# A graph network of two layers on one core: stores of the heads stage on another queue, later constants, ordered loads, and one empty step

## The chip, the cores and the metric

The kernel runs on one NeuronCore of a Trainium2 chip. All times are device microseconds (us) of one execution; the time of a kernel is the median of its runs. The engines are TensorE (PE in the profile, with its weight loads as PEld), VectorE (DVE), ScalarE (ACT), GpSimd (POOL) and SyncE (SP), which issues transfers between the main memory and the on-chip memory. ScalarE can issue transfers too; its transfers stand in a queue of its own.

## What is computed

The input is x, 128 graphs of 128 nodes with 256 channels, and an adjacency matrix for each graph. Layer 0 normalizes x, applies a convolution of width 1 and one of width 17 along the nodes, a message step over soft edges, and a gated update; layer 1 applies five small graph convolutions to groups of the first 25 nodes. Cut to what matters:

```python
h = relu(layernorm(x))
# layer 0
c = relu(bn1(conv1(h)))                  # width 1
c = bn2(conv2(c))                        # width 17, pad 8
x_conv = relu(c + h)
s = h @ w_se.T + b_se
A = exp(-dist(s, s)) * adj
x_nmp = A @ relu(h @ w_msg.T + b_msg)
r, z, n = gates(concat(x_conv, x_nmp), h)  # as in a GRU cell
x = x + (1 - z) * n + z * h
# layer 1: for five groups of nodes, two graph convolutions each
x = x + fused(relu(layernorm(x)), adj)
```

## The kernel before

The 128 graphs are taken in 32 blocks of four (BB = 4, NBLK = 32). The work has three stages.

**Heads** (about 0 to 277 us). The convolution of width 17 is done by a transform along the nodes. Here the weights' spectra are computed (`weight_spectra`, matmuls in line 172), 16 of them, each of four steps, and each written to the tensor `vd` in main memory (line 182, 2176 KB). Beside them run the 32 blocks: load x into a buffer `ln` (line 189, four buffers), statistics (`head_stats`, lines 199 to 205, with a power on GpSimd), normalization (`head_norm`, line 211), transposes and relu (`head_turn`, lines 221 and 222, then a store of the result `ht` to `htd[i]`, line 223), the first convolution (`head_conv1`, matmuls in line 235, bias in line 238), and the spectra of the block (`head_spectra`, line 251, copied to `X`, lines 259 and 261). In this stage the order of every engine is the order of the text (`manual_schedule`). The function `heads` writes this order out; `between()` in it is one step of the weights' spectra. PSUM has eight banks, which this stage takes in rotation: a matmul group can start when the reader of the group eight places before it is done. Constants come from the generator `constants()`: its first part scales the first batch normalization, its second folds it into the weights, its third (`scales(1, ...)`, lines 127 to 132, and line 145) scales the second one. The third part is asked for ahead of `heads`, as are the normalization of block 1 and the statistics of block 2.

**Spectral product** (277 to 457 us). For 68 frequencies p, `spectral` multiplies X by the spectra (lines 321 and 326), after a sum on GpSimd (line 318). The spectra come back from `vd` for four frequencies at a time, in two tiles `v` (line 300, 1024 KB each, five buffers). Results are stored by ScalarE to `yd` and `yrd`. From p = 20 on, every fourth p also calls `gate_steps`, which takes one step of `gate_loads` (the loads of the weights `wms`, `idm`, `bms`, `whh` and `wih` for the next stage, lines 436 to 443) and, at some p, one step of the sums that GpSimd does on these weights. The engines other than GpSimd are ordered by a scheduler here, which may place a load earlier than its text stands.

**Gates** (457 to 1891 us). For each block, `gates` does 28 gate products (line 652; each is two passes per matmul in the profile), with a call of `step()` after each. Steps alternate between the generator `beside_gates(i + 1)`, which prepares the next block, and the second layer's generators. `beside_gates` runs, one piece for each step: the messages (line 538, two pieces), the inverse transform (`conv_out`, two pieces: four matmuls on 16 rows each in line 513 and products in line 517, added to `xc` by VectorE in line 520), the edges' terms, the edges (line 588), the messages' sum (`x_nmp`, line 603), and beside these the pieces of `back(i - 2)` (the end of an earlier block: lines 793 to 834). What is left of it is done in a hook near the end of the gate products. Each product takes one of the eight PSUM banks. VectorE's readers of the products are lines 657 to 673, those of the messages lines 548 to 557.

Of the kernel before, what the change touches and what calls it, by code (L numbers as in the profile page):

```python
# [13 lines left out]
P = 128  # L14
# [12 lines left out]
MW = 130  # L27
# [47 lines left out]
def gnn_kernel(ctx: ExitStack, tc: tile.TileContext, io, out0: bass.AP, out1: bass.AP):  # L75
# [21 lines left out]
    def row(name, n):  # L97

        return bass.AP(tensor=io[name].tensor, offset=io[name].offset, ap=[[0, P], [1, n]])
# [65 lines left out]
    def weight_spectra(pool, c, q, w2):  # L165

        sp = pool.tile([P, LW, WCH], F32, tag="sp", name="sp", bufs=2)
        for t in range(WCH // 8):
            ps = [bank() for _ in range(4)]
            for j in range(2):  # L170
                for r in range(4):
                    nc.tensor.matmul(ps[r][:, j * LW:(j + 1) * LW], w2[32 * r:32 * r + KW, 2 * t + j, :],  # L172
                                     gt[32 * r:32 * r + KW, :], start=True, stop=True)
            for r in range(4):
                o0 = t * 8 + 2 * r
                dst, s = sp[:, :, o0:o0 + 2], ps[r][:, :2 * LW].rearrange("p (j d) -> p d j", j=2)
                if r == 3 and t < WCH // 8 - 1:
                    nc.vector.tensor_copy(dst, s)
                else:
                    nc.scalar.copy(dst, s)  # L180
            yield
        nc.scalar.dma_start(vd[c, q], sp)


    xs, stats, hcs, h1s = {}, {}, {}, {}
# [28 lines left out]
    def head_turn(wk, i):  # L214

        ln = xs.pop(i)
        ht = wk.tile([P, C, T], F32, tag="ht", name="ht", bufs=2)
        for c in range(C):
            ps = bank()
            for b in range(BB):  # L220
                nc.tensor.transpose(ps[:, b * N:(b + 1) * N], ln[:, b, c * P:(c + 1) * P], ident)  # L221
            nc.scalar.activation(ht[:, c, :], ps, AF.Relu)
        nc.scalar.dma_start(htd[i], ht)
        hcs[i] = ht

    def head_conv1(wk, i, h):
# [13 lines left out]
    def head_relu(i, h):  # L240
        hv = h1s[i][:, 2 * h:2 * h + 2, :]
        nc.scalar.activation(hv, hv, AF.Relu)
# [18 lines left out]
                        nc.scalar.copy(dst, s[:, d0:d1])  # L261
                    d0 = d1

    def heads(wk, xk, ahead, X, between):

        for i in range(NBLK + 1):
            if i + ahead < NBLK:
                head_load(xk, ahead, i + ahead, nc.sync)
            if i < NBLK:
                head_conv1(wk, i, 0)  # L270
            between()
            if i < NBLK:
                head_relu(i, 0)
            if i + 3 < NBLK:
                head_stats(wk, i + 3, (0,))
            if i < NBLK:
                head_conv1(wk, i, 1)
            if i + 1 < NBLK:
                head_turn(wk, i + 1)
            if i < NBLK:  # L280
                head_relu(i, 1)
            if i + 2 < NBLK:
                head_norm(i + 2)
            between()
            if i > 0:
                head_spectra(X, i - 1)
            if i % 8 == 7:
                between()
            if i + 3 < NBLK:
                head_stats(wk, i + 3, (1,))  # L290

    def spectral(bp, X, p_from, p_to, amid):

# [68 lines left out]
    with front as es:  # L362
        hk = es.enter_context(tc.tile_pool(name="hk", bufs=1))
        xp = es.enter_context(tc.tile_pool(name="xp", bufs=1))
        X1 = xp.tile([P, C, NP_ - NB, 2, P], F32)
        order = es.enter_context(ExitStack())
        order.enter_context(tc.manual_schedule(engines={nc.gpsimd.engine}))
        early = es.enter_context(ExitStack())
        xe = early.enter_context(tc.tile_pool(name="xe", bufs=1, side="right"))
        X0 = xe.tile([P, C, NB, 2, P], F32)  # L370
        X = X0, X1
        with ExitStack() as ws:

            ws.enter_context(tc.manual_schedule())

            xk = ws.enter_context(tc.tile_pool(name="xk", bufs=1, side="right"))
            wp = ws.enter_context(tc.tile_pool(name="wp", bufs=1))
            ahead = 4
            todo = [(c, q) for c in range(C) for q in range(D // WCH)]
            nc.scalar.dma_start(gt, io["gt"])  # L380
            nc.scalar.dma_start(vec, io["vec"])

            taps = [taps_load(wp, *todo[0], nc.sync, split=4, amid=[lambda: head_load(xk, ahead, 0, nc.sync)])]
            spectra = []

            def some_spectra(k=1):
                for _ in range(k):
                    if not spectra and todo:
                        spectra.append(weight_spectra(wp, *todo.pop(0), taps.pop(0)))
                    if spectra and next(spectra[0], STOP) is STOP:  # L390
                        spectra.pop(0)
                        if len(todo) > 2:
                            taps.append(taps_load(wp, *todo[2], nc.sync))
                        some_spectra()

            constant_loads()
            head_load(xk, ahead, 1, nc.sync)
            taps.append(taps_load(wp, *todo[1], nc.sync))
            for k in range(2, ahead):
                head_load(xk, ahead, k, nc.sync)  # L400
            nc.sync.dma_start(fw, row("fw", 5))
            taps.append(taps_load(wp, *todo[2], nc.sync))
            consts = constants()
            next(consts)
            head_stats(hk, 0)
            some_spectra()
            next(consts)
            head_norm(0)
            some_spectra()
            some_spectra()  # L410
            head_turn(hk, 0)
            head_stats(hk, 1)
            some_spectra()
            head_norm(1)
            head_stats(hk, 2)
            next(consts)
            heads(hk, xk, ahead, X, some_spectra)
            while spectra or todo:
                some_spectra()
        turns.close()  # L420
        banks[:] = [ctx.enter_context(tc.tile_pool(name="psum", bufs=8, space=bass.MemoryType.PSUM, reuse_waits="tile")), None]

        bp = es.enter_context(tc.tile_pool(name="bp", bufs=1, reuse_waits="tile"))
        spectral(bp, (X0, 0), 0, NB, {})
        early.close()
        gw = ctx.enter_context(tc.tile_pool(name="gw", bufs=1, side="right", reuse_waits="tile"))
        idm = gw.tile([P, N], F32)
        wms = gw.tile([P, C, 2, MW], F32)
        bms = gw.tile([P, 2, MW], F32)
        swm = gw.tile([P, 3, MW], F32)  # L430
        wih = gw.tile([P, 2 * C, 3 * D], F32)
        whh = gw.tile([P, C, 3 * D], F32)
        sw = [gw.tile([P, 3, 3, P], F32, name=f"sw{k}") for k in range(3)]

        def gate_loads():
            nc.sync.dma_start(wms, io["wms"].rearrange("(c p) (q o) -> p c q o", p=P, q=2))
            yield
            nc.sync.dma_start(idm, io["idm"])
            nc.sync.dma_start(bms.rearrange("p q o -> p (q o)"), row("bms", 2 * MW))
            for name, w in (("whh", whh), ("wih", wih)):  # L440
                for c in range(w.shape[1]):
                    yield
                    nc.sync.dma_start(w[:, c], io[name][c * P:(c + 1) * P])

        loads, sums = gate_loads(), gate_weights()

        def gate_steps(p):
            next(loads, None)
            if p in (36, 40, 44, 52, 56, 60, 64):
                next(sums, None)  # L450

        amid = {p: lambda p=p: gate_steps(p) for p in range(NB, NP_, 4)}
        spectral(bp, (X1, NB), NB, NP_, amid)
        for _ in sums:
            pass
        order.close()
# [540 lines left out]
    def beside_gates(i):  # L997

        ends = back(i - 2, *back_loads(i - 2)) if i > 1 else iter(())
        if i < NBLK:  # L1000
            parts = messages(i)
            next(parts)
            yield
            next(parts)
            next(ends, None)
            yield
            inverse = conv_out(i) if i else iter(())
            next(inverse, None)
            next(ends, None)
            yield  # L1010
            edge_terms(i)
            next(ends, None)
            yield
            for _ in inverse:
                yield
            edges(i)
            yield
            next(ends, None)
            yield
            yield  # L1020
            yield from x_nmp(i)
        for _ in ends:
            yield
            if i == NBLK:
                yield
# [210 lines left out]
```

## Time and profile before

| | |
|---|---|
| median of 3 runs | 1885.14 us (1882.31 to 1886.73) |
| the profiled execution | 1892.84 us, its span 1891.0 us |
| TensorE busy | 1863.2 us (99%) |
| VectorE, ScalarE, GpSimd busy | 1359.9, 745.7, 666.6 us |
| moved by transfers | 267.98 MB, mean 142 GB/s |
| in the heads stage (100 to 200 us) | 312 GB/s, DMA share 0.86 |
| in the spectral stage (380 to 390 us) | 305 GB/s, DMA share 0.90 |
| a gates block without layer 1 | 37.1 us |

"Busy" counts a matmul from its start to its end, so TensorE can be busy and yet wait inside a row of matmuls. The profile names, for an idle stretch, the instruction whose end came last before it (the releaser). The chain of waits follows the last instruction back to what released it. The granted clock is a share of TensorE's full clock.

### The profile page before, as it was taken

Reading aid. Unit: us, or ns where it says so; the run is one execution under the profiler, and the core shown is the slowest. Engines: PE = TensorE matmul, PEld = TensorE weight load, DVE = VectorE, ACT = ScalarE, POOL = GpSimd, SP = SyncE. Lnnn points to the kernel's source line nnn. Section 1 sums busy time; section 2 is a strip of 40 time slices with the busy share of each in tenths; the row PEclk is TensorE's granted clock in tenths of the full one; section 3 lists DMA queues with packets and bytes.
Section 4 is the critical chain, followed back from the end, with each engine's and each line's share of the span. In section 5 each row is a group of like instructions: output and inputs, shape, how many; then the busy total and the mean of one; then the engine's idle time right before and its main releaser. Section 6 shows DMA issues by size and latency. Waiting matters only on the chain.

```text
span 1891.0 us, 31451 instructions
## 1 busy us (share of the span) xinstructions
PE 1863.2 (99%) x10982; PEld 1601.9 (85%) x10982; DVE 1359.9 (72%) x3312; ACT 745.7 (39%) x1667; POOL 666.6 (35%) x803
## 2 busy tenths in 40 slices
PE   7999999999999999999999999999999999999998
PEld 6888888888888888888788888888788888888787
DVE  6878865455978888888656778887666778888643
ACT  4666651111443334333444433433343343334334
POOL 1111125575344544354312345444312244544200
PEclk8999999999999999999999999999999999999999
DMA  7888778996533233324234432334233333232125
GB/s 264 303 314 318 295 280 281 333 312 236 177 91 76 72 82 90 76 74 111 72 101 113 121 76 71 84 83 111 63 102 97 120 90 84 72 71 69 39 88 155
DMA packets 219421, 267.98 MB, mean 142 GB/s; under 512 B 106211, under 2 KB 182968, under 8 KB 217216
## 3 DMA queue, kind: packets, MB, share of 16 engines
q1 hardware_dynamic: 207167, 195.61, 37.3%
q10 hardware_dynamic: 12096, 70.36, 9.0%
q8 instruction: 88, 1.44, 0.3%
q14 instruction: 70, 0.57, 0.1%
HBM read 169.24 MB, written 96.67 MB: 141 GB/s over the span
## 4 chain that ended last, share of the span: by engine, by line
PE 92%; DMA 3%; DVE 2%; POOL 1%; issue 0%; ACT 0%; SPq 0%; ACTq 0%; DVEq 0%; POOLq 0%
PE bank L652 45%; PE bank L235 6%; PE bank L326 5%; PE bank L980 5%; PE bank L920 5%; PE bank L538 5%; PE bank L517 3%; PE bank L251 3%; PE bank L603 3%; PE bank L321 3%; PE bank L172 2%; PE bank L513 2%; PE bank L221 1%; PE bank L899 1%; PE bank L829 1%; DMA v<-vd 1%
## 5 line engine op out<-in xcount | busy, mean ns | idle before, releaser
L652 PE MATMUL bank<-t,sw 128*128 128x256 f32 x1152 | 291.1, 380 | 0.0
L665 POOL TENSOR_TENSOR u<-u,m 128x256 f32<-128x256 f32 x128 | 94.1, 735 | 499.7 <-ACT m L663 421.4
L652 PEld LDWEIGHTS bank<-t,sw 128*128 128x128 f32 x1152 | 210.6, 190 | 26.7 <-issue 2.3
L652 PE MATMUL bank<-t,wih 128*128 128x256 f32 x768 | 197.2, 379 | 0.0
L652 PEld LDWEIGHTS bank<-t,wih 128*128 128x128 f32 x768 | 143.4, 190 | 19.3 <-DVE u L670 0.5
L235 PE MATMUL bank<-wc,ht 128*128 128x256 f32 x512 | 128.9, 397 | 0.9 <-ACT sp L180 0.9
L318 POOL TENSOR_TENSOR vs<-v 128x256 f32<-128x256 f32 x134 | 98.2, 756 | 76.3 <-PE bank L321 41.3
L561 ACT ACTIVATE msg<-msg 128x512 f32<-128x512 f32 x64 | 37.0, 623 | 207.4 <-DVE msg L557 207.3
L652 PE MATMUL bank<-xc,wih 128*128 128x256 f32 x384 | 117.1, 386 | 0.0
L980 PE MATMUL bank<-w,hh 128*125 128x256 f32 (+9 forms) x480 | 113.8, 380 | 1.9 <-DVE hh L925 1.9
L652 PE MATMUL bank<-t,whh 128*128 128x256 f32 x384 | 114.5, 380 | 0.0
L652 PE MATMUL bank<-xn,wih 128*128 128x256 f32 x384 | 114.2, 379 | 0.0
L235 PEld LDWEIGHTS bank<-wc,ht 128*128 128x128 f32 x512 | 95.6, 196 | 17.1 <-ACT sp L180 1.1
L205 POOL TENSOR_TENSOR rs<-ve,mhalf 128x4 f32<-128x4 f32 x32 | 32.3, 1008 | 220.3 <-DVE ve L203 216.5
L652 PE MATMUL bank<-ht,whh 128*128 128x256 f32 x384 | 109.9, 380 | 0.0
L920 PE MATMUL bank<-ax,w 128*128 128x500 f32 (+8 forms) x416 | 107.0, 396 | 0.1
L980 PEld LDWEIGHTS bank<-w,hh 128*125 128x125 f32 (+9 forms) x480 | 84.3, 178 | 20.4 <-DVE hh L925 2.7
L698 ACT ACTIVATE nn<-nn,vec 128x512 f32<-128x512 f32 x64 | 46.3, 724 | 138.5 <-DVE nn L697 138.5
L315 DVE SCALAR_TENSOR_TENSOR s<-X 128x256 f32<-128x256 f32 x67 | 44.8, 670 | 69.9 <-PE bank L326 69.9
L670 DVE TENSOR_TENSOR u<-bank,u 128x256 f32<-128x256 f32 x128 | 53.5, 418 | 53.9 <-PE bank L652 53.5
L180 ACT COPY sp<-bank 128x272 f32<-128x272 f32 x208 | 66.9, 402 | 55.5 <-PE bank L172 53.9
L920 PEld LDWEIGHTS bank<-ax,w 128*128 128x128 f32 x416 | 69.9, 190 | 19.4 <-issue 12.1
(206 smaller groups left out, 4458.6 us busy)
## 6 DMA issues: line engine op xcount, KB each, us to landing
vd<-sp ACTq DMA_DIRECT2D x16, 2176.0 KB
v<-vd SPq DMA_DIRECT2D x34, 1024.0 KB
w<-in_w_dram SPq DMA_DIRECT2D x40, 512.0 KB
ln<-in_x_dram SPq DMA_DIRECT2D x32, 512.0 KB
htd<-ht ACTq DMA_DIRECT2D x32, 512.0 KB
yd<-ys ACTq DMA_DIRECT2D x32, 512.0 KB
ht<-htd SPq DMA_DIRECT2D x32, 512.0 KB
ym<-yd SPq DMA_DIRECT2D x32, 512.0 KB
```

The costliest lines, as they stand in the source:

```text
L180: nc.scalar.copy(dst, s)
L235: nc.tensor.matmul(pv[:, bb, :], ht[:, c, b * N:(b + 1) * N], wc1[:, c, :], start=c == 0, stop=c == C - 1)
L251: nc.tensor.matmul(ps[:, bb * LW:(bb + 1) * LW], h1[:, 2 * h + bb, c * P:(c + 1) * P], fd, start=True, stop=True)
L318: nc.gpsimd.tensor_tensor(vs[:, c], vr[c], vi[c], op=ALU.add)
L321: nc.tensor.matmul(p1[:, :D], a[:, c], vs[:, c], start=c == 0, stop=c == C - 1)
L326: nc.tensor.matmul(ps[:, k * D:(k + 1) * D], u[:, c], w[c], start=c == 0, stop=c == C - 1)
L517: nc.tensor.matmul(ps[:, b * N:(b + 1) * N], ym[:, 2 * h + b, o * P:(o + 1) * P], idm, start=False, stop=b == 1)
L538: nc.tensor.matmul(ps[:, b, :], d[:, b * N:(b + 1) * N], w, start=True, stop=True)
L652: nc.tensor.matmul(ps, w, d, start=n == 0, stop=n == len(pairs) - 1)
L665: nc.gpsimd.tensor_tensor(got["u4"], got["u2"], got["m5"], op=ALU.add)
L920: nc.tensor.matmul(pv[:, q - q0, :], w1s[k5 + g][:, c, q * P:(q + 1) * P], xv[:, c], start=c == 0, stop=c == C - 1)
L980: nc.tensor.matmul(ps[:n1, :D], hh[:, q, at:at + n1], w2s[k5 + g][:, q, :], start=q == 0, stop=q == HID // P - 1)
```

## The change

Four edits. The stores of the spectra and of `ht` in the heads stage are issued by SyncE in place of ScalarE. The normalization of block 1, the statistics of block 2 and the third part of the constants move from ahead of `heads` into it: into block 0, and (the constants) to the end of block 2; with that, the statistics of block 3 are done in one piece at the end of block 0. The loads of the gate weights are kept in the order of the text among SyncE's instructions. And `beside_gates` has one more step that does nothing, ahead of the first piece of `conv_out`.

```diff
@@ weight_spectra, head_turn @@
-        nc.scalar.dma_start(vd[c, q], sp)
+        nc.sync.dma_start(vd[c, q], sp)
...
-        nc.scalar.dma_start(htd[i], ht)
+        nc.sync.dma_start(htd[i], ht)
@@ heads @@
-    def heads(wk, xk, ahead, X, between):
+    def heads(wk, xk, ahead, X, between, consts):
...
-            if i + 3 < NBLK:
+            if i == 0:
+                head_norm(1)
+            elif i + 3 < NBLK:
                 head_stats(wk, i + 3, (0,))
             if i < NBLK:
                 head_conv1(wk, i, 1)
...
             if i < NBLK:
                 head_relu(i, 1)
+            if i == 0:
+                head_stats(wk, 2)
             if i + 2 < NBLK:
                 head_norm(i + 2)
             between()
...
             if i + 3 < NBLK:
-                head_stats(wk, i + 3, (1,))
+                head_stats(wk, i + 3, (1,) if i else (0, 1))
+            if i == 2:
+                next(consts)
@@ the caller of heads @@
             some_spectra()
-            head_norm(1)
-            head_stats(hk, 2)
-            next(consts)
-            heads(hk, xk, ahead, X, some_spectra)
+            heads(hk, xk, ahead, X, some_spectra, consts)
@@ gate_loads @@
+        def gate_load(to, what):
+            tc.keep_in_program_order(nc.sync.dma_start(to, what))
+
         def gate_loads():
-            nc.sync.dma_start(wms, io["wms"].rearrange("(c p) (q o) -> p c q o", p=P, q=2))
+            gate_load(wms, io["wms"].rearrange("(c p) (q o) -> p c q o", p=P, q=2))
             yield
...
             for name, w in (("whh", whh), ("wih", wih)):
                 for c in range(w.shape[1]):
                     yield
-                    nc.sync.dma_start(w[:, c], io[name][c * P:(c + 1) * P])
+                    gate_load(w[:, c], io[name][c * P:(c + 1) * P])
@@ beside_gates @@
             next(parts)
             next(ends, None)
             yield
+            yield
             inverse = conv_out(i) if i else iter(())
             next(inverse, None)
```

More of the change, by code (lines that the diff above doesn't have):

```diff
@@ L433, in gnn_kernel @@
         sw = [gw.tile([P, 3, 3, P], F32, name=f"sw{k}") for k in range(3)]
+        def gate_load(to, what):
+            tc.keep_in_program_order(nc.sync.dma_start(to, what))
         def gate_loads():
-            nc.sync.dma_start(wms, io["wms"].rearrange("(c p) (q o) -> p c q o", p=P, q=2))
+            gate_load(wms, io["wms"].rearrange("(c p) (q o) -> p c q o", p=P, q=2))
             yield
-            nc.sync.dma_start(idm, io["idm"])
-            nc.sync.dma_start(bms.rearrange("p q o -> p (q o)"), row("bms", 2 * MW))
+            gate_load(idm, io["idm"])
+            gate_load(bms.rearrange("p q o -> p (q o)"), row("bms", 2 * MW))
             for name, w in (("whh", whh), ("wih", wih)):
```

## The prediction

> **What bounds the kernel now.** The page first: its busy table says that TensorE is the bound, with 27.8 us of the span in which it does nothing. So a change can win only in those 27.8 us, or where TensorE is busy but slower than it could be. The waits of TensorE, and of its weight loads, come next.
>
> ```profile
> PE 1863.2 (99%) x10982; PEld 1601.9 (85%) x10982; DVE 1359.9 (72%) x3312; ACT 745.7 (39%) x1667; POOL 666.6 (35%) x803
> ...
> PE bank L321 <- POOL vs L318: 3.3, 1, 3.3
> PE bank L513 <- DMA yr<-yrd: 3.0, 1, 3.0
> PE bank L172 <- DVE h L238: 2.9, 1, 2.9
> ...
> PEld bank L652 <- DVE nh L667: 9.2, 26, 0.4
> PEld bank L513 <- DVE u L660: 7.6, 23, 0.3
> ```
>
> Columns: us in total, times, longest. Three single waits of 3 us stand beside two small ones that come once in nearly every block. The small ones hardly show in TensorE's busy time, because a matmul held up counts as busy. Third, the chain of waits around the single ones (start, us, what), and the table of stretches for the granted clock.
>
> ```profile
> 22.87 1.00 POOL rs L205
> 23.88 0.68 POOL bnrs L129
> ...
> 25.21 0.61 DVE h L238
> ...
> 25.86 1.29 PE bank L172 x16
> 27.15 3.71 PE bank L235 x8
> ...
> 37.44 2.05 PE bank L251 x16
> 39.49 1.73 PE bank L235 x8
> ```
>
> ```profile
> 340.21 11.63 DMA v<-vd
> ...
> 351.91 0.73 POOL vs L318
> ...
> 353.38 3.36 PE bank L326 x8
> ```
>
> After each idle stretch the same work takes twice as long: L235 x8 3.71 us against 1.73 at 39.49, L326 x8 3.36 against 1.73 in the steady chain. The stretches 26 to 37 and 353 to 357 us have a granted clock of 0.55 and 0.57. Fourth, the timeline of TensorE around line 513, in block 1 and in a block of the middle, and the chain after it:
>
> ```profile
> 485.15 0.71 PE L513 MATMUL bank<-idr,yr 16*128 16x256 f32 x8
> ```
>
> ```profile
> 1109.11 1.06 PE L513 MATMUL bank<-idr,yr 16*128 16x256 f32 x8
> ```
>
> ```profile
> 1119.12 3.25 PE bank L652 x14
> ```
>
> The same eight instructions take 0.71 us where their four PSUM banks are free and 1.06 where one waits for VectorE's line 660: 0.35 us lost. L652 x12 is 2.59 us everywhere, so x14 should be 3.02; here it is 3.25, the wait for line 667: 0.23 us.
>
> [...] This run shows 0.33 us of ScalarE for a store, and nothing yet on both kinds in one queue. [...]
>
> **Heads' stores by SyncE.** Removed from ScalarE: 32 + 16 issues of 0.33 us, 16 us. No wait of TensorE for ScalarE in this stage exceeds 1.1 us in all, so this is worth 0. Added on SyncE: the same issues, and two waits. Store htd(i+1) waits for the relu of block i+1 (about 1.1 us after its transposes); behind it is the x load of block i+5, released by those transposes: 1.5 us later. vd was complete one step earlier, so it doesn't block. In the queue, though, the load can stand behind htd 0.52, vd 2.23 and taps 0.52 MB: with its own 0.52, 3.8 MB; at 310 to 430 GB/s (measured in the stage and at 255 to 258 us) 8.8 to 12.2 us, after 1.5 us. VectorE's stats need it 13.7 us after the transposes (93.2 to 106.9 us), and TensorE stands it 1.3 us longer (h of line 238 ends at 101.1, its bank is needed at 102.4). It fits, hardly. At the end, the second v load waits behind htd of block 31: 268.7 instead of 265.5 us, needed at 277. I take 1 us lost; bounds 0 and the slower rival.
>
> **Second constants behind the first blocks.** Up to 21.9 us nothing moves on TensorE. VectorE now runs h(0,0) at 19.4 (conv1 just done) to 20.0, a copy to 20.4, norm(1) (1.38) to 21.8, h(0,1) to 22.5, stats(2) with ve (2.3) to 24.9, POOL's pow to 26.0, norm(2) to 27.4, copy to 27.75, stats(3) to 30.1, h(1,0) to 30.7. TensorE, at full clock: transposes of block 1 to 22.9, L172 to 23.6, L235 to 25.35, L172 to 26.0, L235 to 27.95, L221 to 28.85. The next L172 takes the bank that h(1,0) reads: 1.9 us idle, to 30.7; then 31.4; L251 needs h(1,1), at 32.7 (half a stats and 0.6 us later), and ends at 34.3. Before, it ended at 39.49: 5.2 us gained. What is late next is VectorE, with stats of blocks 2 and 3 in a row. The scales moved to the end of block 2 cost VectorE about 2.4 us there (bnve to brz, 22.70 to 25.12); h(3,0) is then at 46.2, its bank wanted at 47.4: hidden, and up to 1 us if not. Bounds: 7.9 us without the idle 1.9 and 0.8; 0 if 1.9 us idle halves the clock again as long as before (it lost 5 us).
>
> **Gate weights' loads in text order.** In the program as built, the second whh load and the first wih load leave the place ahead of the second v of step 28, and the other three wih loads go one to each group of four steps. That v can't start earlier (its buffer is released by step 23, at 340.2). Two loads of 0.39 MB ahead of it at 400 GB/s are 2.0 us, so 11.63 becomes 9.6; TensorE starts at 350.6 instead of 352.7, idle 1.2 us against 3.3 and with no halved clock. The three wih loads issued at 344.5 to 349.2 also shared these 11.6 us, so it may be all of it. Value of all: 3.3 idle, plus 0.27 (L321 x2 0.70 for 0.43) and 1.63 (L326) and 0.05: 5.3. I take 4.7; bounds 2.1 and 5.3. The spread loads add 1.0 us of DMA to each 10.4 us group, in which a tenth is free (share 0.88 to 0.90 from 370 to 400 us). The sums on GpSimd come at step 40 and later: hidden.
>
> **The empty step.** It puts line 513 behind two more gate products (12 L652, 2.6 us). Its four banks are then those that VectorE lines 660, 555, 556 and 557 read; in the block at 1109 us these end by 1110.3, and line 513 comes at 1111.8: no wait. Gain 0.35 x 23 = 8.0 us. Next the banks of the second half: line 520 for it now comes after n2, the statistics of line 819 and hn, by my sums at 1117.0 to 1117.8; the first matmuls of nn that take its bank come at 1118.4: no wait either, and line 667's bank is no longer taken there. Gain 0.23 x 25 = 5.8. The edges' bank (hn's) is free at 1117.0, wanted at 1117.4. Twelve steps of the generator instead of eleven still fit in the thirteen ahead of the hook. So 13.8; bounds: 16 (the three longer waits at 817, 893 and 1333 us, 0.7 each, also gone), and -5 if a wait of 0.6 comes with each of 30 blocks in place of these.
>
> **Sum.** 5.2 + 4.7 + 13.8 - 1.0 = 22.7 us. Own time of the profiled execution 1892.84 (span 1891.0 and 1.8 around it), so 1870.1; it lay 7.7 us over the median 1885.14, and the same change of the median gives 1862.4.
>
> **Rivals.** (a) The wait at line 513 only moves: the margins of 0.4 to 0.6 us at hn's and line 520's banks are eaten by ScalarE, which must copy n1 and relu xc first. Against: five of six margins are larger. Then 8.9 us are left: 1876. (b) The idle 1.9 us at 29 us halves the clock and the v load stays late: 5.2 and 2.6 us less, 1870. (c) Slower: stores and loads in one queue. From the point where an x load comes 15.0 us or later after its buffer's transposes, each us is TensorE's; at 3 us for 14 of 16 vd stores, 42 us: 1885 + 42 - 23 = 1904. For it: the DMA share is 0.82 to 0.86 in this stage. Against: the sums above. It decides over the rest from 1.6 us for each store. (d) The change does little: the steady waits are filled by others and the single ones return elsewhere: 1885.
>
> **Numbers.** Forecast 0.62, (a) 0.20, (b) 0.08, (c) 0.07, (d) 0.03. 0.2% (3.8 us) is about what a measurement of this kernel can tell from no change. Faster 0.90, same 0.03, slower 0.07. Range 1855 (7.9 + 5.3 + 16 gives 1856) to 1877, which takes in (a) and (b).
>
> **What would show it.** Line 513 x8 at 0.7 us in all blocks and no row of its weight loads for line 660; L652 x14 at 3.02 us; the first L251 ending near 34 us, clock 1.00 from 26 to 37; no PE wait for POOL at line 321. Wrong if PE or VectorE waits for x loads at line 199 before 260 us, or if line 588, 652 or 829 shows a new wait in 20 blocks and more. The wait for yr at 462 us stays.

## The result, and the profile after

The changed kernel takes 1865.39 us (median of 4 runs, 1865.10 to 1866.29) where the kernel before takes 1885.33 in the runs beside it: ratio 0.9897, 95% interval 0.9880 to 0.9914, 19.9 us less. In a second comparison, with other runs of both, the ratio was 0.9901 (0.9886 to 0.9916). The forecast was 1862.4, in a range of 1855 to 1877. The changed kernel's profiled execution spans 1864.5 us and is 0.9 us above its median; the one before spans 1891.0 and lay 7.7 above. The profiled spans therefore differ by 26.5 us, 6.6 more than the medians.

Lines 321, 326, 513, 588, 652, 667 and 829 of before are lines 327, 332, 519, 594, 658, 673 and 835 of after. The busy table of the changed kernel:

```profile
PE 1843.8 (99%) x10982; PEld 1592.3 (85%) x10982; DVE 1361.9 (73%) x3312; ACT 737.0 (40%) x1668; POOL 652.9 (35%) x803
```

TensorE is still the bound and runs the same 10982 instructions, but it is "busy" for 19.4 us less: most of what went was hidden in busy time. Its idle time fell only from 27.8 to 20.7 us. The waits of TensorE in the changed kernel (us in total, times, longest):

```profile
PE bank L519 <- DMA yr<-yrd: 3.2, 1, 3.2
...
PE bank L172 <- DVE h L238: 2.0, 1, 2.0
PE bank L251 <- DVE h L238: 1.0, 2, 0.6
```

No row for POOL at line 327: the stall at step 28 (frequency p = 28 of the spectral product) is gone. The wait for yr stays. The front still waits for h, now in three pieces. The timeline of TensorE in the changed kernel (start, us, and in brackets the idle time before, with what ended it) shows the front and one block of the middle:

```profile
31.50 0.74 PE L172 MATMUL bank<-gt,w 17*128 17x136 f32 x16 [1.96 <-DVE h L238]
...
33.50 3.09 PE L251 MATMUL bank<-fd,h 128*128 128x136 f32 x12 [0.59 <-DVE h L238]
...
42.60 2.12 PE L251 MATMUL bank<-fd,h 128*128 128x136 f32 x16
```

```profile
1131.96 0.71 PE L519 MATMUL bank<-idr,yr 16*128 16x256 f32 x8
```

The reader is to see two things. Line 519 takes 0.71 us also in the middle of the run, where it took 1.06. And twelve L251 take 3.09 us after two short idle times, while sixteen take 2.12 at 42.60: the clock is halved again behind the idle 1.96 and 0.59 us (granted 0.50 from 33.45 to 36.86 us). The chain of waits of the changed kernel (start, us, what) confirms the steady blocks:

```profile
1095.50 0.64 PE bank L519 x8
...
1110.77 10.36 PE bank L658 x48
...
1132.03 0.64 PE bank L519 x8
```

48 products in 10.36 us are 0.216 each, the undisturbed price: the wait of 0.23 us for the bank of line 667 is gone too. From one line 519 to the next are 36.53 us; before it was 37.09. One sign that the prediction named for being wrong is there, on VectorE: the statistics of line 199 wait for x loads, which in the kernel before they never did:

```profile
DVE st L199 <- DMA ln<-in_x_dram: 2.9, 3, 1.2
```

TensorE has no wait between 60 and 270 us, so these waits stay hidden.

### The profile page after: what moved, and what is told of

It is laid out like the page before. It is cut to its first block, busy times and chain, and to the rows that moved or that the text cites. A ratio compares the mean times of both kernels' runs of the same rounds, so it can differ in the third digit from the quotient of the medians.

```text
span 1864.5 us, 31417 instructions
## 1 busy us (share of the span) xinstructions
PE 1843.8 (99%) x10982; PEld 1592.3 (85%) x10982; DVE 1361.9 (73%) x3312; ACT 737.0 (40%) x1668; POOL 652.9 (35%) x803
## 4 chain that ended last, share of the span: by engine, by line
PE 90%; DVE 4%; DMA 2%; POOL 2%; SPq 1%; issue 1%; ACT 1%; ACTq 0%; DVEq 0%; POOLq 0%
PE bank L658 43%; PE bank L332 6%; PE bank L235 6%; PE bank L926 5%; PE bank L986 5%; PE bank L544 4%; PE bank L251 4%; PE bank L523 3%; PE bank L327 3%; PE bank L609 3%; PE bank L172 2%; PE bank L221 1%; PE bank L905 1%; DMA nt<-in_adjN_dram 1%; PE bank L835 1%; PE bank L519 1%
## 5 line engine op out<-in xcount | busy, mean ns | idle before, releaser
L235 PE MATMUL bank<-wc,ht 128*128 128x256 f32 x512 | 126.0, 390 | 0.0
L235 PEld LDWEIGHTS bank<-wc,ht 128*128 128x128 f32 x512 | 93.8, 193 | 15.1 <-issue 0.3
L986 PEld LDWEIGHTS bank<-w,hh 128*125 128x125 f32 (+9 forms) x480 | 84.3, 178 | 18.8 <-DVE hh L931 1.0
L669 ACT COPY m<-bank 128x256 f32<-128x256 f32 x128 | 47.3, 369 | 104.5 <-PE bank L658 104.5
L926 PEld LDWEIGHTS bank<-ax,w 128*128 128x128 f32 x416 | 69.9, 190 | 19.4 <-issue 12.3
```

Of the source, the lines that this page charges most:

```text
L235: nc.tensor.matmul(pv[:, bb, :], ht[:, c, b * N:(b + 1) * N], wc1[:, c, :], start=c == 0, stop=c == C - 1)
L926: nc.tensor.matmul(pv[:, q - q0, :], w1s[k5 + g][:, c, q * P:(q + 1) * P], xv[:, c], start=c == 0, stop=c == C - 1)
L986: nc.tensor.matmul(ps[:n1, :D], hh[:, q, at:at + n1], w2s[k5 + g][:, q, :], start=q == 0, stop=q == HID // P - 1)
```

## The experiments

Twelve runs. First each part alone on the kernel before, then each of three parts taken out of the changed kernel, then second looks and doses. The state of knowledge when each expectation was written is in its text. They were made in three comparisons of four kernels, each with its own runs of the kernel before (medians 1885.14, 1887.40 and 1886.36 us), against which the ratios stand.

### Stores alone

```
-        nc.scalar.dma_start(vd[c, q], sp)
+        nc.sync.dma_start(vd[c, q], sp)
-        nc.scalar.dma_start(htd[i], ht)
+        nc.sync.dma_start(htd[i], ht)
```

> The kernel before with the heads' two kinds of store given to SyncE and nothing else. Theory (the three other parts each remove a wait of their own, and the stores are worth nothing): within 2 us of the kernel before, no wait of line 199 for x loads, the second v load of step 28 as late as before (TensorE idle about 3.3 us at line 321). Rival 1 (the stores carry a part of the gain, because ScalarE is free of 48 issues): 3 us or more faster, with fewer waits of TensorE for ScalarE between 40 and 270 us. Rival 2 (stores and loads in one queue cost something that the other parts hide): 3 us or more slower.

Measured 1885.41 us, ratio 0.9998 (0.9991 to 1.0005). The theory holds on the time. Two of its details fell. VectorE waited for x loads at line 199, 3.4 us in 4 times, though TensorE did not wait between 60 and 270 us. And the second v load wasn't "as late as before": this execution waited only 0.5 and 0.7 us for POOL at line 321, the first sign that this stall isn't the same in each execution.

### Constants alone

The diff's edits in heads and in what calls it, nothing else; its core:

```
-            head_norm(1)
-            head_stats(hk, 2)
-            next(consts)
...
+            if i == 2:
+                next(consts)
```

> The kernel before with the second constants behind the first blocks and nothing else. Theory: the first L251 ends at 36 to 37 us instead of 39.5, TensorE idle 1.9 to 2 us at line 172 and again 0.6 us at line 251, clock down to about 0.8 from 30 to 40 us; 2 to 3.5 us faster. Rival (the place at the front is a gain only because the stores have left ScalarE): the first L251 ends at 38 us or later, less than 1.5 us faster.

Measured 1888.98 us, ratio 1.0016 (1.0006 to 1.0025): slower, which neither theory expected. The timeline of TensorE in this kernel:

```profile
32.83 3.09 PE L251 MATMUL bank<-fd,h 128*128 128x136 f32 x12 [0.59 <-DVE h L238]
...
41.85 1.43 PE L251 MATMUL bank<-fd,h 128*128 128x136 f32 x10
```

```profile
349.83 1.02 PE L327 MATMUL bank<-vs,X 128*128 128x256 f32 x2 [2.63 <-POOL vs L324]
350.64 1.91 PE L332 MATMUL bank<-v,s 128*128 128x256 f32 x4
```

(The view of the second group ends after ten of its sixteen matmuls.) The front does what the theory said: the first L251 ends at 35.9. But the second group of L251 (the 17th, of block 1) starts at 41.85. In the first profile of before it started at 45.30, but in three other executions with the old front and the stores on ScalarE it starts at 41.82, 42.43 and 42.91, and in two with the old front and the stores on SyncE at 40.62 and 40.69. So the new front is earlier only against that first profile. Why this kernel is slower, and not merely the same, isn't shown. At step 28 this execution has a long stall with a halved clock behind it (1.91 us for four L332, 1.03 elsewhere).

### Gate loads alone

The diff's gate_load and its uses, nothing else:

```
+        def gate_load(to, what):
+            tc.keep_in_program_order(nc.sync.dma_start(to, what))
```

> The kernel before with the gate weights' loads in text order and nothing else. Theory: no wait of TensorE for POOL at line 321, TensorE busy throughout from 340 to 360 us at full clock, 4.5 to 6 us faster. Rival (the loads only fit because the stores and the front have moved the time of the spectral steps against the transfers): a wait of 1 us or more stays at line 321 or at line 326, less than 3 us faster.

Measured 1882.38 us, ratio 0.9984 (0.9977 to 0.9992), 1.5 to 4.3 us faster. There is no wait of TensorE at line 321 or 326 and no idle time from 340 to 360 us, as the theory said; the size is smaller than it said, and the rival's remaining wait isn't there either. So the stall is gone, but in the usual execution it costs less than in the first profile of before.

### Empty step alone

```
             yield
+            yield
             inverse = conv_out(i) if i else iter(())
```

> The kernel before with the empty step ahead of the inverse and nothing else. Theory: line 513 x8 takes 0.71 us in all blocks (section of eight 0.95 us instead of 1.29), L652 x14 loses its 0.22 us, the steady block takes 36.5 us instead of 37.1, 12 to 15 us faster: the largest of the four parts. Rival (a wait of the same size comes back at hn's bank, line 829, or at line 517): 3 to 8 us faster, with a row of 20 or more such waits. If the four parts are independent, their gains add to the 19.9 us between the two kernels within 3 us.

Measured 1870.81 us, ratio 0.9921 (0.9906 to 0.9937), 14.3 us by the medians. The theory holds, and this one line is some three quarters of the whole. The four ratios add to 0.81% where the whole has 1.03 and 0.99%. The half widths of the four intervals, added as squares, are 0.21%: the missing 4 us aren't shown to be an interaction (by the medians some 7 are missing).

### Without the stores, without the constants, without the gate order

Each is the changed kernel with one part put back as it was before. The stores:

```
-        nc.sync.dma_start(vd[c, q], sp)
+        nc.scalar.dma_start(vd[c, q], sp)
-        nc.sync.dma_start(htd[i], ht)
+        nc.scalar.dma_start(htd[i], ht)
```

> The changed kernel with the heads' stores given back to ScalarE. The four parts alone measured 0, +3.8, -2.8 and -14.3 us, which add to -13.3, not to the -19.9 of the whole, so two parts help each other. Theory A (the stores are worth nothing alone, but with the constants moved ScalarE's issues hold TensorE at line 235 for 1 to 1.5 us between 100 and 150 us): 1867 to 1869 us, with a row 'PE bank L235 <- ACT sp' of over 1 us. Theory B (the whole missing 6.5 us is between the stores and the constants): 1871 to 1873 us. Theory C (what is missing lies between the constants and the gate loads): within 1 us of the changed kernel, 1865.4.

Measured 1868.45 us, ratio 0.9900 (0.9884 to 0.9915): the same as the changed kernel's 0.9897 and 0.9901. Theory B falls. The wait that theory A named is in its profile, the only one of TensorE between 60 and 270 us, where the changed kernel has none in either of its profiles:

```profile
PE bank L235 <- ACT sp L180: 1.7, 1, 1.7
```

The constants, and with them the first statistics and norms as before:

```
+            head_norm(1)
+            head_stats(hk, 2)
+            next(consts)
...
-            if i == 2:
-                next(consts)
```

> The changed kernel with the second constants back ahead of the heads. Theory A (in the usual execution the front is set by VectorE and by the phase of the halved clock, so that the place of the constants is worth about nothing; alone it lost 3.8 us because the later step 28 met its transfers in a bad phase): within 1.5 us of the changed kernel. Theory B (as in the profiles of the two kernels: 2.9 us gained at the front): 1868 to 1869 us. Theory C (they are worth -3.8 here too): about 1861.6 us.

Measured 1866.46 us, ratio 0.9891 (0.9873 to 0.9909). Theory A fits best: the constants' place is worth nothing that these runs can tell. The interval alone decides little: theory B's 1868 to 1869 us (0.9908 to 0.9913 of the first comparison's 1885.33) stands at its upper edge and theory C's 1861.6 (0.9874) at its lower one.

The gate loads:

```
-                    gate_load(w[:, c], io[name][c * P:(c + 1) * P])
+                    nc.sync.dma_start(w[:, c], io[name][c * P:(c + 1) * P])
```

and so for the three other loads of gate_loads.

> The changed kernel with the gate weights' loads free of the text order again. Theory A (the stall of TensorE at step 28 is of different length from execution to execution, since what shares the transfer with the second v load differs; the text order removes it always): 3 to 6 us slower than the changed kernel, a wait for POOL at line 327 of 1 to 3 us, and a wider spread of the times. Theory B (2.8 us as alone): 1868 us with a spread no wider than that of the changed kernel. Theory C (with the other parts the step comes at another time and the order is worth nothing): within 1 us of the changed kernel.

Measured 1870.43 us (1868.96 to 1875.29), ratio 0.9914 (0.9896 to 0.9932), some 3 us above the changed kernel's by the ratios. The spread decides nothing: 6.3 us here, and 1.2 and 5.8 us in the two comparisons that had the changed kernel. The intervals overlap; the wait itself is plain, in the timeline of TensorE:

```profile
347.95 0.70 PE L327 MATMUL bank<-vs,X 128*128 128x256 f32 x2 [1.70 <-POOL vs L324]
```

### The kernel before, a second profile

> The kernel before once more, for a second profile. Its first profiled execution lay 7.7 us over the median of its times. Theory A: this one is nearer to the median, with the first L251 ending 2 to 3 us earlier (as in the two profiles of kernels that leave the front alone) and a shorter stall at line 321, step 28. Theory B: the front and the stall are as in the first profile, and the difference lies after 500 us, in the tail.

Its execution took 1885.77 us. Theory A holds. TensorE's waits in it, and its timeline:

```profile
PE bank L172 <- DVE h L238: 2.1, 1, 2.1
...
PE bank L321 <- POOL vs L318: 0.8, 2, 0.6
```

```profile
34.50 2.12 PE L251 MATMUL bank<-fd,h 128*128 128x136 f32 x16
...
42.43 2.12 PE L251 MATMUL bank<-fd,h 128*128 128x136 f32 x16
```

In the first profile these two groups start at 37.37 and 45.30. So 2.9 us of the front in the profile that the prediction was made from belonged to that execution, and the stall of 3.3 us at step 28 with its halved clock (granted 0.50 from 353.31 to 356.72 us) isn't in each execution: here TensorE was idle 0.2 us at step 28 and 0.6 at step 32.

### The changed kernel, a second profile

> The changed kernel once more, beside the three below on the same chip, and for a second profile. Theory A (most of the difference of the two first profiles before 500 us was one slow execution of the kernel before, and the halved clock after the idle 2 us at 29 us belongs to the new front): 1864 to 1868 us; the first L251 ends at 36 to 37 us and block 1's second L235 no earlier than in the profiles of kernels with the old front. Theory B (the new front is faster by 2 to 3 us when it is not disturbed): the first L251 ends at 34 to 35 us.

Measured 1868.19 us (1866.07 to 1871.85). TensorE's timeline in it:

```profile
33.98 2.49 PE L251 MATMUL bank<-fd,h 128*128 128x136 f32 x12 [0.59 <-DVE h L238]
...
43.12 2.12 PE L251 MATMUL bank<-fd,h 128*128 128x136 f32 x16
```

Theory A holds on the front: the first L251 ends at 36.5 and the 17th starts at 43.12, no earlier than with the old front (40.62 to 42.91, leaving out the first profile of before).

### A smoother front, and the addend of block 0 later

```
             if i == 0:
                 head_norm(1)
-            elif i + 3 < NBLK:
-                head_stats(wk, i + 3, (0,))
+            elif i + 2 < NBLK:
+                head_stats(wk, i + 2, (1,) if i > 1 else (0,))
...
-            if i == 0:
-                head_stats(wk, 2)
-            if i + 2 < NBLK:
+            if i < 2:
+                head_stats(wk, i + 2, (1,) if i else (0, 1))
+            if i + 2 < NBLK and i != 1:
                 head_norm(i + 2)
...
-            if i + 3 < NBLK:
-                head_stats(wk, i + 3, (1,) if i else (0, 1))
+            if i == 1:
+                head_norm(3)
+            if i and i + 3 < NBLK:
+                head_stats(wk, i + 3, (0,))
...
         if held[0] == 3:
-            for _ in conv_out(0):
-                pass
-            gate_inputs(0, (0,))
             while 0 not in lrs:
...
+        if held[0] == 1:
+            for _ in conv_out(0):
+                pass
+            gate_inputs(0, (0,))
```

> The changed kernel with two edits. First, each half of the statistics of blocks 3 and later comes half a block later on VectorE, so that h(1,0) follows the norm of block 2 at once. Second, block 0's spectral addend (lines 519 and 523) comes two gate products later, with block 0's edges ahead of it. Theory A (the idle 2 us at 29 us and the halved clock behind it are what took the front's gain): no wait at line 172 for h, full clock from 20 us on, the first L251 ends at 32 to 33 us instead of 36.6 and the 17th L251 starts 3.5 to 5 us earlier; the wait for yr falls from 3.2 to 1.5 to 2.3 us; 4 to 6.5 us faster than the changed kernel. Theory B (VectorE is the bound of the first three blocks, so that the wait only moves to line 221 for the norm of block 3 or to line 235): the 17th L251 starts less than 1.5 us earlier, 1 to 2.5 us faster in all.

Measured 1863.88 us (1862.41 to 1866.33), ratio 0.9877 (0.9863 to 0.9891), 4.3 us below the changed kernel's 1868.19 of the same comparison, and the fastest kernel of this study; the two intervals just overlap. The timeline of TensorE in it:

```profile
33.22 1.66 PE L251 MATMUL bank<-fd,h 128*128 128x136 f32 x12 [0.29 <-DVE h L238]
...
40.69 2.12 PE L251 MATMUL bank<-fd,h 128*128 128x136 f32 x16
```

```profile
454.95 0.66 PE L584 MATMUL bank<-ident,lr 128*128 128x128 f32 x2 [3.20 <-DVE lr L577]
```

The wait at line 172 is gone, twelve L251 take 1.66 us, and the 17th L251 starts 2.4 us earlier than in the second profile of the changed kernel: between the two theories. But the executions differ ahead of that: here the halved clock of the start lasted to 24.5 us, in the two profiles of the changed kernel to 19.8 and 21.0. Two other kernels with the changed kernel's front had a start like this one (to 25.5 us without the stores, to 25.0 with two empty steps); their 17th L251 start at 45.12 and 46.40, so that like against like the first edit brings 4.4 to 5.7 us, which is theory A. The second edit gained nothing in this execution: the wait for yr became a wait of the same length for the edge terms, which VectorE finishes at the same moment. From the first message product to block 1's addend both kernels take 29.1 us (with the clock halved for 10.2 us of it here and for 6.8 us in the changed kernel). The wait for yr had covered this one.

### All gate loads behind the v loads of step 28

```
                     nc.sync.dma_start(v[c], vd[c, :, :, 2 * p:2 * p + 8, :].rearrange("q i d o -> i q d o"))
+                amid.get(-p, lambda: None)()
...
-            next(loads, None)
+            if p < 28:
+                next(loads, None)
...
+        amid[-28] = lambda: list(loads)
```

> The changed kernel with all six loads of whh and wih (2.4 MB) issued at once, directly behind the two v loads of step 28, where the text order spreads them over six groups of four steps. Theory A (what costs is that loads stand ahead of the v load in SyncE's order): no wait at line 327, within 1 us of the changed kernel. Theory B (what costs is that the loads are in transfer beside it, whether they are ahead or behind): v lands 9 us or more after its issue, a wait of 1 to 3 us for POOL at line 327, 2 to 6 us slower. A wait at step 32 instead of 28 would speak for A with a longer queue.

Measured 1873.14 us, ratio 0.9928 (0.9914 to 0.9941), 5 us slower. Step 28 has no wait, though 2.4 MB stand directly behind its v loads; the wait has gone to step 32, whose v loads stand behind those 2.4 MB. SyncE's own rows, and TensorE's timeline, in this kernel:

```profile
328.09 7.42 SPq L306 DMA_DIRECT2D v<-vd  x2
335.56 1.06 SPq L440 DMA_DIRECT2D whh<-in_whh_dram  x2
336.67 6.40 SPq L440 DMA_DIRECT2D wih<-in_wih_dram  x4
344.86 14.25 SPq L306 DMA_DIRECT2D v<-vd  x5
```

```profile
359.77 0.70 PE L328 MATMUL bank<-vs,X 128*128 128x256 f32 x2 [3.12 <-POOL vs L325]
```

That is theory A with the longer queue: what stood ahead in SyncE's order delayed a v load, what stood behind didn't. The first v load of step 32 was issued at 344.86 us here, at 336.52 in the changed kernel. (The load of step 32 itself landed 13.3 us after its issue; what part of that is due to the transfers ahead of it isn't shown.)

### Two empty steps

```
             yield
             yield
+            yield
             inverse = conv_out(i) if i else iter(())
```

> The changed kernel with a second empty step ahead of the inverse: thirteen steps where thirteen have room. Theory A (the gain is the removal of a wait, which is gone with one step): line 519 x8 takes 0.71 us and the steady block 36.5 us as with one, and the total is within 2 us of the changed kernel or up to 6 us slower if the later end of x's inverse makes TensorE wait for xc, e or xn once a block (0.2 us x 30). Theory B (the instructions gain by standing later as such, a step more gains more): 5 us or more faster.

Measured 1883.02 us, ratio 0.9979 (0.9970 to 0.9988): nearly the whole gain is lost, 14.8 us against the changed kernel of the same comparison. Theory B falls, and theory A's allowance of 6 us was too small, because the wait came back at the old place and not at xc, e or xn. Beside it stand three new waits of TensorE at line 544, each 1.6 to 1.7 us, for VectorE's reader of a message bank (line 554): 5.0 us, where the changed kernel has 0.3. The weight loads' waits of TensorE in this kernel, its chain, and VectorE's timeline:

```profile
PEld bank L519 <- DVE o L673: 5.2, 24, 0.6
```

```profile
1108.27 1.10 PE bank L519 x8
...
1145.25 1.10 PE bank L519 x8
```

```profile
1108.19 0.42 DVE L673 TENSOR_TENSOR o<-bank,u 128x256 f32<-128x256 f32 x1 [1.11 <-POOL u L671]
```

Two gate products further, line 519 wants the bank that line 673 reads, and line 673 is held 1.11 us by the sum on GpSimd: 1.10 us instead of 0.64, and a block of 36.98 us. Line 519 isn't helped by standing later; it is helped by standing at a place in the rotation of banks whose readers are early.

## Why the prediction was right, and where not

**The empty step, 13.8 us: right, by its own mechanism.** Alone 14.3 by the medians (11.9 to 17.7 from the interval). In the traces, from the end of the spectral product to the end of the program are 1430.9 to 1433.2 us in the five profiles without this step and 1415.4 to 1417.8 in the eight with one: 15.8 us between the means. Both terms were found: line 519 at 0.71 us, the products at 0.216 each, together 0.56 us for each block, against 0.35 and 0.23. None of the new waits that the rivals placed at lines 588, 652 or 829 came. The announced sign "no row of its weight loads for line 660" held, but a row of 0.3 us for line 575 stands in its place, and beside it line 519 still takes 0.71: a row of that size in the weight loads' waits is no loss by itself. The x8 time decides.

**The gate loads, 4.7 us: right in mechanism, the term was too large.** The stall is absent in every profile of a kernel with the text order alone or with all parts. It is worth 2.8 us (1.5 to 4.3) alone and about 3 taken out. The mis-sized number is the 11.63 us of the v load in one profiled execution. Without the text order TensorE's idle time at this step was 3.3, 0.2, 0.5, 2.6, 3.2 and 1.7 us in six profiles (before twice, stores alone, constants alone, empty step alone, without the gate order). With what followed it, a halved clock in three of the six (before, constants alone, empty step alone), the step took 5.2, 0.5, 0.8, 4.6, 5.1 and 2.0 us more than its usual 2.59 (from the first matmul of step 28 to that of step 29, by their starts in the trace): 3.0 in the mean, close to the measured gain.

**The constants, 5.2 us: wrong.** The walk through VectorE was right to 0.8 us (h(1,0) forecast to end at 30.7, measured 31.45; idle 1.9, measured 1.96). What failed is the step "first L251 ... ends at 34.3. Before, it ended at 39.49: 5.2 us gained", in two ways. Behind the idle 1.96 and 0.59 us the granted clock was 0.50, so that it ended at 36.6; this was kept as rival (b), for 0.08, and should have been in the forecast, since the prediction's own profile showed a granted clock of 0.50 for 10.2 us behind an idle 2.9 us. (In five profiles with this front, those of the changed kernel, the constants alone, without the stores and without the gate order, the twelve L251 behind the two idle times took 2.49 to 3.09 us, against 1.66 with the smoother front.) And 39.49 was that of a slow execution; the second profile of before has 36.6. Measured at the 17th L251, the new front isn't earlier, and which of the two is ahead goes with the moment at which the halved clock of the start ended. Where it ended between 18.8 and 21.0 us, the old front stands at 41.8 to 45.3 (four profiles) and the new one at 41.9 to 43.1 (five). Where it lasted to 24.2 us or longer, TensorE was slow enough not to wait at line 172 with the old front (40.6 and 40.7), while the new front has its idle 1.8 or 2.0 us in any case (45.1 and 46.4) and, without the stores, slow work behind it once more (3.05 us for twelve L251). That would make the constants' new place a loss in the mean, as they measured alone; with two profiles on each side it isn't shown.

**The stores, 1 us lost: wrong in sign at most, and small.** The prediction's "It fits, hardly" is about what the traces show. The sign of rival (c) came on VectorE, which waited for x loads at line 199 in seven of the eight profiles with the stores on SyncE (1.9 to 3.6 us, in three or four waits of at most 1.4) and in none of the six with the stores on ScalarE. By the prediction TensorE bears 1.3 us of such lateness, and it had no wait between 60 and 270 us in any of the eight. So what (c) priced didn't come, but the loads were close to it. In profiles with the stores on ScalarE, the stretch from the 17th to the 257th L251 took 122.1 to 123.9 us (six profiles); with the stores on SyncE 120.6 to 121.3 (eight). The prediction gave 0 for ScalarE's relief; in this stretch it is 1 to 3 us, and TensorE's wait of 0.9 to 1.7 us for sp at line 235 is in all six of the first kind and in none of the eight. Yet the times of the stores alone show no gain (0.9991 to 1.0005). Where it is given back stays open.

**The sum.** 22.7 forecast, 19.9 measured. The constants' 5.2 were lost, the gate loads' term was some 2 too large, and the stores' 1 us didn't have to be paid. With the empty step's 14.3, the gate loads' 2.8 and 0 for the other two, 17.1 us are accounted for; the remaining 2.8 lie within the uncertainty of the parts. The traces place the gain: between the second profile of before and the first of the changed kernel (spans 1884.0 and 1864.5) the heads are 1.6 us shorter, the spectral product 1.3 and all that follows 16.6. The prediction took its durations from an execution 7.7 us above the median and carried the difference over whole. The front's 2.9 us and the excess of step 28's stall over its mean, 2.2 us, were in those 7.7 us and couldn't be won again from the median. The sum came out as near as it did by luck in part: of the 9.9 us that it put on single waits some 7 were not there, and the empty step's larger gain and the stores that cost nothing made up for about half. What isn't luck is the 13.8, six tenths of the forecast, which rested on some 25 repetitions of each of two waits that are the same in each execution. Of the rivals, (a) is excluded by line 519 at 0.71 us in the steady blocks, (c) by TensorE's empty list of waits between 60 and 270 us, (d) by the time; (b)'s first half happened.

## What to carry to other kernels

A wait that recurs in each of many blocks is a firm number even from a single profile; a wait that comes once near a transfer should be read in a second profile of the same kernel before it is priced. When an instruction waits for its bank, count which reader holds each bank in the rotation and look for the place whose readers are early: one step further won 14 us here, two steps lost them again. And a single wait that is about to be removed may cover another that ends at the same time: follow the second chain (here the edge terms behind yr) to its own end first.

## What was not expected of the hardware

In these profiles the halving of the clock doesn't follow the length of an idle time alone. At steps 28 and 32 an idle 1.70 us (without the gate order) and an idle 3.12 us (all gate loads behind) left the work behind them undisturbed (1.03 us for four L332 after the one and for four L333 after the other), while 2.63 us with the constants alone halved it (1.91 for four L332), and at the front of the changed kernel 1.96 and 0.59 us within 4 us did so, too. The traces show more. In the first profiles of the two kernels, from the end of the halved clock of the start to 40 us before the end of the program, the moments at which the granted clock changes lie multiples of 3.41 us apart: at 25.63, 35.87, 353.31, 356.72, 465.95 and 472.77 us before, at 33.45, 36.86, 456.70 and 463.53 us after. Here are two of the idle times in stretches of that length, counted from the changes in each profile, first 2.63 us with the constants alone, then 3.12 us with all gate loads behind (stretch, its length and TensorE's busy time in us; the 1.00 or 0.50 ahead of the last two numbers is the granted clock):

```profile
346.66:350.07 3.41, 0.78 (x4) 0.38 (x3) 0.69 (x1) 0.00 (x0) 1.01 (x2) 1.00 1.05 395
350.07:353.48 3.41, 3.41 (x9) 2.70 (x9) 0.86 (x1) 0.37 (x1) 3.41 (x6) 0.50 1.05 386
```

```profile
354.94:358.35 3.41, 1.71 (x8) 1.15 (x7) 1.23 (x2) 0.02 (x1) 0.70 (x1) 1.00 1.07 387
358.35:361.76 3.41, 1.99 (x9) 1.78 (x10) 0.39 (x1) 0.37 (x1) 2.76 (x5) 1.00 1.10 366
```

The shorter idle time lies whole in one stretch and leaves it 0.78 us of work, and the clock of the next is 0.50; the longer one is cut into 1.70 and 1.42 us, and the clock stays 1.00. In the first profiles of the two kernels, with the same part of the program cut in this way, the five stretches directly ahead of a halved clock had 2.00 to 3.01 us of idle time, and no other at full clock had more than 0.89. At the front of the changed kernel the 2.00 us are the sum of two short waits. Why the clock changes as it does isn't shown. The first halved clock of the heads, under which eight L235 took up to 3.78 us instead of 1.99, ended at 18.8 us in the first profile of the kernel before and at 25.5 without the stores.

With the heads' stores on SyncE some x loads came late for VectorE (2.9 us in three waits, the longest 1.2, in the first profile of the changed kernel), which none did in that of the kernel before; the stage also ran 1 to 3 us faster with the stores on SyncE, which may have a part in it. With the gate loads ahead of it in SyncE's order a v load was issued at 344.86 us, 8.3 us later than in the changed kernel.
